# A two-layer graph transformer: one more feed-forward block in seven products, the next layer's keys one chunk later, the last empty attention steps spaced

## The chip, the cores and the metric

The kernel runs on one core of one Trainium2 chip. The time is the device time of one execution, in microseconds (us). Smaller is better. Five engines work side by side, each through its own instructions in their written order: PE (TensorE, matrix products), ACT (ScalarE, activations and copies with a scale), DVE (VectorE, elementwise work and reductions), POOL (GpSimd, here mostly indirect transfers and small powers) and SP (SyncE, here only transfers).

## The reference

There are 2708 tokens of 512 values and a 0/1 adjacency matrix, sparse enough that no token has more than 24 neighbours. Two layers of the same form follow each other; cut to what matters, one is:

```python
q, k, v = ((h @ W.T + b).reshape(n, 8, 64) for W, b in ((Wq, bq), (Wk, bk), (Wv, bv)))
scores = jnp.einsum('nhd,mhd->hnm', q, k) / jnp.sqrt(64.)
scores = jnp.where(mask[None] == 0, -1e9, scores)
ctx = jnp.einsum('hnm,mhd->nhd', jax.nn.softmax(scores, -1), v).reshape(n, 512)
h1 = layer_norm(h + ctx @ Wo.T + bo, ln1_g, ln1_b)
ff = jax.nn.relu(h1 @ W1.T + b1) @ W2.T + b2          # W1: 2048 x 512, W2: 512 x 2048
h2 = layer_norm(h1 + ff, ln2_g, ln2_b)
```

Everything is 32-bit floating point.

## The kernel before, in words

**Tokens and blocks.** The tokens are sorted by their number of neighbours and cut into 22 tiles of 128 (the last, tile 21, holds 20). Two tiles make a block, and a layer runs over 11 blocks, `k` from 0 to 10. The order of the tiles is fixed in a list; the last block holds tile 21 and tile 0, and tile 0 has the longest neighbour lists (22).

**What a block does.** The main loop (L2078 to L2183) takes one block at a time through 16 chunks, `f` from 0 to 15. Chunk `f` computes 128 of the 2048 hidden values for the block's 256 tokens: four products into `pf` on PE (each of 256 columns), then a relu from `pf` to `ft` on ACT. The second matrix is applied some chunks later. The work of other stages is hung on these chunks by hand, so that PE always has something to do. All engines are scheduled by hand: each instruction stands on its engine where the loop issues it.

**Two forms of the second product.** In the plain form (`feed_forward`, L1548) chunk `f-3` is multiplied with its 128 x 512 part of W2 for both tiles: two products of 512 columns per chunk. In the seven-product form (`feed_forward_by_seven`, L1734) two chunks and two tiles make a 2 x 2 block product, done by the Strassen-Winograd scheme: seven products of 256 columns in place of eight. It has 7 such pairs of chunks, `j` from 0 to 6, and the last two chunks in the plain way. `sums(j)` (four DVE operations, L1746 to L1749) forms the sums of the relu outputs that the scheme needs; it is issued in chunk `2j+2`. `products(j)` (L1751) issues the seven products at the end of chunk `2j+5`, that is, after everything else that the loop hangs on that chunk. The first of the seven needs no sums; the second needs the result of L1748. `ask_forms` (L1725) fetches the three preformed pieces of W2 for each pair with transfers on SP. `FORMED = (1, 3)` (L60) says for each layer after which block the seven-product form begins: in layer 0 blocks 2 to 9 have it, in layer 1 blocks 4 to 9. Before it begins, `prepared` (L2086) lays out its buffers in the place of Wq, `form_in` (L2135, L2137) puts one difference of W2's parts in the place of a part of W2, and `places_of_psum` (L2088) goes from three PSUM buffers for `pf` (tag `f`) and three for everything else (tag `g`) to two and two, with two for the sums of products.

**What is hung on the chunks.** In the order of one pass of the loop: first the chunk's own products and relu, and then

- in layer 1, a step of `ended` for the block before (the last layer norm and the store), at the chunks in `TAILS`;
- in layer 0, a step of `keys_values` (L1858) for the block before, at chunks 5, 6, 7 and 8 (L2101, L2102): the first step turns the block's two tiles on PE (`flip`, L1349: transposes into two PSUM buffers `tp` of tag `g`, and four ACT copies for each from there to `zT`, L1354). The second and third step project one tile each to keys and values of layer 1 (L626, 8 + 8 PE instructions, `k` and `v` in the same two PSUM buffers), with a DVE add and an ACT copy, and store `zT` and the tile through SP. The fourth writes the keys and values by an indirect transfer on POOL (`put`);
- at chunks 10 to 14, the output projection and the first layer norm of the next block (`attended`), whose tiles must have come out of the attention by then: `until(...)` (L2106, L2111) forces the rest if they have not;
- at chunk 15 the next block is turned for its own first products;
- `advance` (L2120) runs steps of the attention.

**The attention** (`attend`, L1908) is a generator of steps in the order of the tiles. A step takes up to two neighbours of each token of a tile: `weights` multiplies the gathered keys with the queries and sums over each head (DVE, L1156 and L1162). One step later `weigh` takes the exponentials (ACT, L1175), multiplies the values of the second neighbour by them (8 ACT operations, L1182) and those of the first (DVE, L1188), and adds them up (DVE, L1195). For the last step of a tile, `sums` follows one step after that (DVE, L1203 to L1218) and `divided` another one later (8 ACT operations, L1226, into `cx`). Behind the first block's two tiles and at the end of the layer stand three empty steps that only let this tail run out. Each step has a price, 0.5 or 1 for one or two neighbours and 0.2 for an empty one (L1950); `advance` hands out credit by `PACE` or, in seven-product blocks, `PACE7`, and runs steps while credit is left and fewer than three finished tiles wait.

## Time and profile before

| | |
|---|---|
| median of 3 runs | 1817.57 us (1815.81 to 1818.39) |
| the profiled execution, its time | 1817.08 us |
| its span, first to last instruction | 1815.1 us |
| PE, busy share of the span | 99% |
| DVE, ACT, POOL | 81%, 55%, 47% |

The time of an execution is about 2 us above the span of the same execution, the part before the first and after the last instruction. A busy share is a mean over stages that differ; a busy PE means that some product was under way. Two kinds of view carry the argument. A table of stages gives, for stretches of time, the busy time of each engine; the stretches used here run from the first relu of one block to the first relu of the next, so that each is the length of a block. A timeline lists the instructions of an engine in order of time, like neighbours merged into one row: start, duration, engine, line, operation, out<-in, shapes, count, and in brackets how long the engine had been idle and for what. One matrix product in 32-bit floating point appears as two PE instructions.

### The profile page before, as it was taken

How to read it: one execution, taken by the hardware profiler on the slowest of the kernel's cores; microseconds unless marked ns; L12 is line 12 of the kernel's file. 1: busy time of each engine (PE TensorE's matmuls, PEld its weight loads, DVE VectorE, ACT ScalarE, POOL GpSimd, SP SyncE). 2: the span in 40 equal slices, each digit the busy share in tenths (PEclk: the TensorE clock that was granted, in tenths of full speed). 3: DMA queues.
4: the chain of work that ended last, by engine and by line, in shares of the span. 5: the costliest groups of instructions: out<-in, count | busy, mean ns of one | idle time of the engine just before them, and what ended most of it. 6: DMA issues, size and time to landing. Idle time of an engine off the chain costs nothing. (4 is left out here: it accounts for less than half of the span.)

```text
span 1815.1 us, 23887 instructions
## 1 busy us (share of the span) xinstructions
PE 1791.5 (99%) x6839; PEld 1214.6 (67%) x6839; DVE 1463.3 (81%) x2599; ACT 1001.1 (55%) x3397; POOL 855.4 (47%) x830
## 2 busy tenths in 40 slices
PE   9999999999999999999999999999999999999997
PEld 4444456666777867777677644666666888788786
DVE  4987778988989889799896267988888899989933
ACT  5771436645555555555653104677776677767631
POOL 3333755534454544454540132556665665655312
PEclk9999999999999999999999999999999999999999
DMA  9997987757676675666752777967867787877531
GB/s 335 369 344 252 374 284 245 230 181 241 203 238 220 203 259 192 208 220 202 241 194 73 242 285 272 319 193 256 279 186 263 243 264 237 293 225 234 173 94 36
DMA packets 186728, 426.74 MB, mean 235 GB/s; under 512 B 20550, under 2 KB 83898, under 8 KB 186584
## 3 DMA queue, kind: packets, MB, share of 16 engines
q0 software_dynamic: 76992, 264.49, 44.0%
q1 hardware_dynamic: 99434, 139.01, 22.5%
q10 hardware_dynamic: 10158, 21.61, 3.1%
q8 instruction: 56, 0.92, 0.2%
q14 instruction: 88, 0.72, 0.1%
HBM read 357.13 MB, written 57.11 MB: 228 GB/s over the span
## 5 line engine op out<-in xcount | busy, mean ns | idle before, releaser
L1119 POOL DMA_INDIRECT kv<-kv_d,listed x420 | 526.0, 1252 | 307.2 <-DVE acc L1195 145.8
L1780 PE MATMUL pf<-hT,w 128*128 128x256 f32 x1792 | 407.2, 379 | 2.1 <-ACT ft L1791 2.1
L1780 PEld LDWEIGHTS pf<-hT,w 128*128 128x128 f32 x1792 | 339.2, 190 | 59.2 <-issue 11.0
L1182 ACT ACTIVATE kv<-kv,p 128x64 f32<-128x64 f32 x1232 | 311.0, 335 | 5.0
L1156 DVE TENSOR_TENSOR kv<-kv,q 128x1024 f32<-128x1024 f32 (+1 forms) x222 | 257.1, 1158 | 14.1 <-DMA q<-q_d,ident_i 10.9
L1162 DVE TENSOR_REDUCE sc<-kv 128x16 f32<-128x1024 f32 (+1 forms) x222 | 258.0, 1162 | 7.6
L1195 DVE TENSOR_TENSOR acc<-acc,kv 128x1024 f32<-128x1024 f32 (+2 forms) x178 | 205.6, 1155 | 49.6 <-ACT kv L1182 36.9
L1596 PEld LDWEIGHTS pf<-hT,w 128*128 128x128 f32 x1024 | 178.5, 190 | 55.3 <-issue 34.6
L1596 PE MATMUL pf<-hT,w 128*128 128x256 f32 (+1 forms) x1024 | 214.6, 357 | 0.1
L1791 ACT ACTIVATE ft<-pf,b 128x256 f32<-128x256 f32 x168 | 78.1, 466 | 214.1 <-PE pf L1780 211.4
L1569 PE MATMUL a<-w,ft 128*128 128x512 f32 x416 | 194.6, 592 | 0.0
L1175 ACT ACTIVATE p<-sc,listed 128x8 f32<-128x8 f32 x420 | 103.6, 295 | 127.9 <-DVE sc L1162 116.5
L1281 POOL TENSOR_TENSOR rd<-va,mhalf 128x1 f32<-128x1 f32 (+1 forms) x48 | 43.8, 913 | 230.8 <-DVE va L1279 230.7
L626 PE MATMUL o<-wo,cT 128*128 128x512 f32 x336 | 151.0, 593 | 0.3 <-ACT cT L1354 0.3
L1188 DVE TENSOR_TENSOR kv<-kv,p 128x512 f32<-128x512 f32 (+1 forms) x178 | 123.6, 694 | 4.8 <-ACT p L1175 4.5
L1569 PEld LDWEIGHTS a<-w,ft 128*128 128x128 f32 x416 | 77.7, 190 | 57.5 <-issue 52.0
L626 PEld LDWEIGHTS o<-wo,cT 128*128 128x128 f32 x336 | 63.4, 190 | 69.3 <-issue 59.6
L1331 POOL TENSOR_SCALAR va<-sq 128x1 f32<-128x1 f32 (+1 forms) x40 | 17.2, 429 | 188.4 <-ACT xb L1324 101.9
L751 DVE MAX8 tops<-code 128x8 f32<-128x247 f32 (+2 forms) x242 | 78.8, 400 | 28.0 <-ACT code L746 27.9
L1226 ACT ACTIVATE cx<-acc,su 128x64 f32<-128x64 f32 (+1 forms) x352 | 88.2, 333 | 11.2 <-DVE su L1218 6.2
L1182 ACT ACTIVATE acc<-kv,p 128x64 f32<-128x64 f32 (+1 forms) x352 | 88.8, 335 | 1.4
L746 ACT ACTIVATE code<-aj 128x1354 bf16<-128x1354 int32 (+1 forms) x44 | 73.5, 1724 | 23.7 <-POOL aj L740 19.0
(258 smaller groups left out, 2793.8 us busy)
## 6 DMA issues: line engine op xcount, KB each, us to landing
forms<-form_d SPq DMA_DIRECT2D x294, 128.0 KB, 3.8
aj<-in_adj SPq DMA_DIRECT2D x42, 677.0 KB, 6.3
kv_d<-kvs ACTq DMA_DIRECT2D x21, 512.0 KB, 7.4
h<-ln_b POOLq DMA_DIRECT2D x41, 256.0 KB, 7.0
xg<-in_xT SPq DMA_DIRECT2D x19, 512.0 KB, 8.0
w<-in_W SPq DMA_DIRECT2D x16, 512.0 KB, 6.4
kv<-kv_d,listed POOLq DMA_INDIRECT x420, 6.5
zT_d<-zT SPq DMA_DIRECT2D x22, 256.0 KB, 5.3
```

Source lines behind the costliest of these rows:

```text
L626: nc.tensor.matmul(o[:r], xs(c), wm[:, c, :], start=(c == 0), stop=(c == NC - 1))
L1119: return nc.gpsimd.indirect_dma_start(out=to, out_offset=None, in_=table[:, :], in_offset=bass.IndirectOffsetOnAxis(ap=s, axis=0), bounds_ ...
L1156: nc.vector.tensor_tensor(kv[:r, :c, :DM], kv[:r, :c, :DM], self.q[:r].unsqueeze(1).to_broadcast([r, c, DM]), ALU.mult,)
L1162: nc.vector.tensor_reduce(self.sc[:r, s0 : s0 + c, :], kv[:r, :c, :DM].rearrange("p s (h d) -> p s h d", d=DK), AX.X, ALU.add,)
L1175: nc.scalar.activation(p[:r, s, :], self.sc[:r, s, :], AF.Exp, bias=minus[:r, g, s : s + 1])
L1182: nc.scalar.activation(to[:, i, hd], kv[:r, i, DM + h * DK : DM + (h + 1) * DK], AF.Copy, scale=p[:r, s0 + i, h : h + 1],)
L1188: nc.vector.tensor_tensor(to[:, 0, :].rearrange("p (h d) -> p h d", d=DK), kv[:r, 0, DM:].rearrange("p (h d) -> p h d", d=DK), p[:r, s0, : ...
L1195: nc.vector.tensor_tensor(self.acc[:r, :c, :], self.acc[:r, :c, :], kv[:r, :c, DM:], ALU.add)
L1226: nc.scalar.activation(cx[:r, hd], self.acc[:r, 0, hd], AF.Copy, scale=self.su[:r, h : h + 1])
L1569: nc.tensor.matmul(a[:r, cols], fts[f][:, c0 : c0 + r], self.w2[f // 2][:, f % 2, cols], start=(f == 0), stop=(f == NFC - 1),)
L1596: nc.tensor.matmul(pf[:, :w], self.w1[f // 2][:, c, f % 2 * P : f % 2 * P + P], hT[:, c, :w], start=(c == 0), stop=(c == NC - 1),)
L1780: nc.tensor.matmul(pf[:, :W], self.w1[j][:, c, f % 2 * P : f % 2 * P + P], hT[:, c, :], start=(c == 0), stop=(c == NC - 1),)
```

## The change

Three lines change.

```diff
-FORMED = (1, 3)
+FORMED = (1, 2)
...
             if t3 and t3[-1]:
                 got[t3[0].g] = t3[0].divided()
-            yield c / SLOTS if step else 0.2
+            yield c / SLOTS if step else 0.2 if g == order[1] else 1.0
...
                 if tail and f in TAILS[k > FORMED[n] + 1]:
                     next(tail)
-                if f in (5, 6, 7, 8) and behind:
+                if behind and more <= f - 5 < 4 + more:
                     next(behind)
```

The first lets the seven-product form begin at block 3 of layer 1, its fourth, and moves with it what prepares it: the buffers and the differences of W2 one block earlier (block 2 and the start of block 3), the two PSUM buffers of each kind from block 3 on, and the pace of `PACE7` for the attention in block 3.

The second gives the three empty steps at the end of a layer a price of 1.0 each; those behind the first block keep 0.2.

In the third, `more` is true for all blocks but the last, and counts as 1: the four steps of `keys_values` stand at chunks 6, 7, 8 and 9 in blocks 1 to 9 of layer 0, and at 5 to 8 in block 10 as before. Layer 1 has no such steps.

## The prediction

> **What bounds the kernel now.** I read the page first, then who waited for whom, then the blocks as stages, last the timelines of chunks 4 to 7.

> ```profile
> span 1815.1 us, 23887 instructions
> PE 1791.5 (99%) x6839; PEld 1214.6 (67%) x6839; DVE 1463.3 (81%) x2599; ACT 1001.1 (55%) x3397; POOL 855.4 (47%) x830
> ```

> PE lacks 23.6 us of its span, so a change pays only by fewer products or by fewer of PE's waits, and each new wait of PE is paid in full. One wait that the third edit is about leads the list of PE's waits:

> ```profile
> PE tp L1349 <- DVE h L1290: 3.1, 4, 1.0
> ```

> Layer 0's blocks 2, 3, 4, 5 and 6 as stages (length, then PE busy):

> ```profile
> 395.47:472.05 76.58, 75.73 (x311) 1.00 0.67 219
> 472.05:548.92 76.87, 75.89 (x311) 1.00 0.66 223
> 548.92:624.38 75.46, 75.46 (x311) 1.00 0.68 227
> 624.38:700.88 76.50, 75.71 (x311) 1.00 0.65 212
> 700.88:777.38 76.50, 75.72 (x311) 1.00 0.64 208
> ```

> A block without waits takes 75.46; blocks 2 and 3 lose 1.1 and 1.4.

> **Edit 1, the seven products.** Layer 1's block 3 (plain, now), 4 (seven), 6, 8 and 9 (length, then PE, PEld, DVE, ACT and POOL busy, granted clock, share of the DMA engines):

> ```profile
> 1341.94:1405.65 63.71, 63.71 (x225) 41.13 (x224) 53.23 (x73) 46.55 (x170) 39.05 (x37) 1.00 0.74 251
> 1405.65:1466.49 60.84, 60.84 (x271) 49.87 (x270) 53.97 (x91) 44.72 (x161) 38.01 (x34) 1.00 0.80 262
> 1527.34:1588.91 61.57, 61.24 (x271) 49.77 (x270) 58.37 (x102) 40.86 (x145) 37.37 (x33) 1.00 0.79 257
> 1650.02:1712.80 62.78, 61.82 (x271) 49.60 (x270) 59.92 (x102) 44.75 (x162) 30.41 (x30) 1.00 0.68 219
> 1712.80:1770.85 58.05, 58.05 (x272) 47.60 (x271) 28.53 (x70) 23.50 (x73) 10.37 (x14) 1.00 0.32 78
> ```

> Block 3 goes from 63.71 to 60.84: **-2.9 us**. It takes PE's products over from block 4 as they are: 49 products of 256 columns and four wide ones' worth in place of 32 wide ones of 512, 3.5 wide ones fewer at some 0.86 each. Block 4 is itself the first of its form and pays nothing for the change of buffers. Block 3 adds 28 DVE sums and 21 fetches on SP, and moves seven fetches one block up; DVE (54 of 61) and the transfers (0.80) carry that in block 4. Its pace sums to 10.0 in place of 11.1; by the prices, 10 steps run in block 3 in place of 12, and block 9, where DVE is busy for 28.53 of 58, gets 3 in place of 1. In between every step stands one or two chunks later. Blocks 6 and 8 show what an unlucky place costs, 0.7 and 1.9 over 60.84; shifted steps can lose these 2.7 or find them again: -2.7 to +2.7, and I take 0, as blocks of the same form lie on both sides.

> PEld, the weight loads, grows from 41.13 to 49.87 while the block gets shorter. [...]

> **Edit 3, the keys one chunk later.** What does the turning of the block wait for, and what is next? Block 2, chunk 5:

> ```profile
> 403.91 0.60 PE L1349 MATMUL tp<-ident,h 128*128 128x128 f32 x4
> 405.75 0.28 DVE L1748 TENSOR_TENSOR forms<-forms,ft 128x128 f32<-128x128 f32 x1
> 405.85 0.60 PE L1769 MATMUL a<-forms,ft 128*128 128x256 f32 x2
> ```

> The second tile's turn waits for the block before's layer norm on DVE. Unhindered, as in block 7 below, the first product follows the first turn by 0.87; here by 1.94, in block 3 by 2.07. Removed by the move: 1.07 + 1.20 = **-2.3**. But products(0), issued at the end of chunk 5, now comes in the place of the turn, and needs DVE too: its second product takes the result of L1748, which DVE computes right behind the same layer norm. Nothing makes DVE earlier. Blocks 3, 5 and 8:

> ```profile
> 480.49 0.60 PE L1349 MATMUL tp<-ident,h 128*128 128x128 f32 x4
> 482.45 0.28 DVE L1748 TENSOR_TENSOR forms<-forms,ft 128x128 f32<-128x128 f32 x1
> 482.56 0.60 PE L1769 MATMUL a<-forms,ft 128*128 128x256 f32 x2
> ```

> ```profile
> 632.81 1.04 PE L1349 MATMUL tp<-ident,h 128*128 128x128 f32 x8
> 633.41 0.28 DVE L1748 TENSOR_TENSOR forms<-forms,ft 128x128 f32<-128x128 f32 x1
> ```

> ```profile
> 861.41 1.04 PE L1349 MATMUL tp<-ident,h 128*128 128x128 f32 x8
> 862.14 0.28 DVE L1748 TENSOR_TENSOR forms<-forms,ft 128x128 f32<-128x128 f32 x1
> ```

> Block 7 gives the pace of the array:

> ```profile
> 785.81 1.04 PE L1349 MATMUL tp<-ident,h 128*128 128x128 f32 x8
> 786.68 0.60 PE L1769 MATMUL a<-forms,ft 128*128 128x256 f32 x2
> 789.71 1.89 PE L1780 MATMUL pf<-hT,w 128*128 128x256 f32 x8
> 791.43 3.60 PE L626 MATMUL k<-wk,zT 128*128 128x512 f32 x8
> ```

> Two turns 0.87, seven products 3.03 (0.43 each), a chunk's `pf` 1.72. So the second product is wanted 0.43 after the row of the turn: block 2 at 404.34, L1748 ends at 406.03: 1.7 lost. Block 3: 482.73 - 480.92 = 1.8. Block 5, and 6 which has its length: 633.69 - 633.24 = 0.45 each. Block 8: 862.42 - 861.84 = 0.6. Block 7: none. First waits: **+5.0**. Bounds: 0 if DVE came early, 5.0 as it stands.

> The second thing is ACT's queue. Now the copies of `zT` stand behind the relu of chunk 5 and ahead of chunk 5's attention step. After the change they stand behind that step and the relu of chunk 6. And `k` needs the PSUM buffer that the four copies of the first tile read (two buffers of tag `g`), so all four must be done. Block 7, ACT:

> ```profile
> 787.45 2.14 ACT L1354 ACTIVATE zT<-tp,bo 128x128 f32<-128x128 f32 x8
> 790.01 0.49 ACT L1175 ACTIVATE p<-sc,listed 128x8 f32<-128x8 f32 x2 [0.42 <-DVE sc L1162]
> 792.46 2.00 ACT L1226 ACTIVATE cx<-acc,su 128x64 f32<-128x64 f32 x8
> 794.37 0.45 ACT L1791 ACTIVATE ft<-pf,b 128x256 f32<-128x256 f32 x1
> ```

> The step starts when DVE has its scores, whatever stands ahead of it, and ends with the relu of chunk 6 at 794.82. Four copies take half of 2.14: `zT` is there at 795.9. On PE, `k` comes after products(0), `pf`, two turns, `pf`: 785.81 + 3.03 + 1.72 + 0.87 + 1.72 = 793.15. Lost: 2.7. Today the same copies are ready in time, ahead of the step. Block 8 has the same eight scalings in chunk 5, block 3 has none there:

> ```profile
> 870.59 0.45 ACT L1791 ACTIVATE ft<-pf,b 128x256 f32<-128x256 f32 x1
> ```

> ```profile
> 488.99 0.46 ACT L1791 ACTIVATE ft<-pf,b 128x256 f32<-128x256 f32 x1
> ```

> Block 8: copies done 871.04 + 1.05 = 872.1; PE 861.41 + 7.34 + the 0.6 already lost = 869.35: 2.75. Block 3: 490.5 against 480.49 + 7.34 + 1.8 = 489.65: 0.85. In blocks 2 and 5 the step would start at its scores:

> ```profile
> 408.58 1.22 DVE L1162 TENSOR_REDUCE sc<-kv 128x16 f32<-128x1024 f32 x1
> ```

> ```profile
> 636.25 1.22 DVE L1162 TENSOR_REDUCE sc<-kv 128x16 f32<-128x1024 f32 x1
> ```

> A step without scalings is 2.45 (790.01 to 792.46), relu and copies 0.45 + 1.05: block 2 done at 409.80 + 3.95 = 413.75 against 403.91 + 7.34 + 1.7 = 412.95: 0.8; block 5 at 641.4 against 640.6: 0.8, and 6 the same. Blocks 1, 4, 9 I leave at 0. Second waits: 2.7 + 2.75 + 0.85 + 0.8 x 3 = **+8.7**. Lower bound 0, if ACT came in time; upper bound about +10, if blocks 4 and 9 pay the 0.8 of their neighbours.

> Queues it is moved past: two stores per tile on SP now stand ahead of the fetches of products(1), and wait only for `zT`; `put` on POOL stands behind one more step's gathers and waits for the same ACT copy, the gathers behind it being three steps ahead of use: 0. The last two attention steps of chunk 8 in blocks 5 and 6 keep their distance to the keys' end, so the waits there stay. Edit 3: -2.3 + 5.0 + 8.7 = **+11.4**.

> **Edit 2, the empty steps.** Layer 0, block 9, chunks 9 to 11, and the stage:

> ```profile
> 969.61 1.99 PE L1780 MATMUL pf<-hT,w 128*128 128x256 f32 x8
> 971.18 0.20 DVE L1218 RECIPROCAL su<-su 128x8 f32<-128x8 f32 x1
> 971.42 2.02 ACT L1226 ACTIVATE cx<-acc,su 128x64 f32<-128x64 f32 x8 [2.54 <-DVE flags L1951]
> 974.01 1.52 PE L621 MATMUL o<-wo,cT 128*20 128x512 f32 x8 [2.41 <-ACT cT L1354]
> ```

> ACT stands for 2.54 on the sums of tile 0, and tile 21's copy, behind it, holds PE for 2.41. With the price of 1.0 the three empty steps fall to chunks 8, 10 and 11, the last by force, just ahead of tile 0's own turn. The wait of 2.41 goes; but PE reaches tile 0's turn at 971.4 + 1.5, when the sums, moved behind four DVE operations of 0.28 and a bit, are done at 972.6 and the scalings at 974.6: 1.7. Net **-0.7** (-2.4 to +1). In layer 1 the tail ended at chunk 7 and cost nothing; now, one step later too, it ends at chunk 11: relu 0.45 and scalings 2.0, of which the product of tile 21 covers 1.5, and the drain before the relu: **+1.2** (0 to 2).

> **Sum**: -2.9 + 11.4 - 0.7 + 1.2 = +9.0 on the profiled execution's 1817.08: 1826.1. It lies 0.49 under the median, so **1826.6**.

> **The rivals.**
> *A, the keys move costs nothing (faster).* If DVE's norm at the head of a block ended 2 us earlier, sums and scores would be there and both kinds of waits fall away: 1817.6 - 2.9 - 2.3 + 0.5 = 1812.9. It decides from the point where L1748 ends within 0.43 of the end of chunk 5's products. For it: blocks 4 and 7 are there already. Against it: DVE's chain from the block's end to L1748 has no instruction of the keys in it.
> *B, only the waits on DVE come*, since ACT takes the copies in time: 1826.6 - 8.7 = 1817.9, no change. For it: blocks 2, 3, 5 and 6 hang by 0.8. Against: blocks 7 and 8, by 2.7.
> *C, a long wait slows the array.* Each stretch quoted shows a granted clock of 1.00, with the gap of 2.41 too:

> ```profile
> 928.43:1004.30 75.87, 73.46 (x315) 55.10 (x314) 51.63 (x96) 30.62 (x111) 14.08 (x12) 1.00 0.34 110
> ```

> Two waits of 2.7 are the first longer ones inside layer 0's blocks. If each brought as much again: 1826.6 + 5.4 = 1832. [...]
> *D, edit 1 does not do what it says*: block 3 finds the waits of blocks 6 and 8 too, 2.6 over 60.84, and its gain is gone: 1829.

> **How the numbers follow.** About 0.2% (3.6 us) is what a measurement of this kernel can tell from no change. The forecast has 0.62, with its own range 1821.5 to 1830.5 from the bounds of edit 1 and the second waits. A 0.16, B 0.13, C 0.04, D 0.05. A lies beyond 0.2% faster, B within, the others slower; a tail of the forecast falls within: faster 0.17, same 0.15, slower 0.68. The range reaches from 1814.5, above A, to 1830.

> **What would show it.** In layer 0's blocks 2, 3, 5, 6, 8: `c<-forms` waits for DVE L1748, and no turn waits for L1290. In blocks 7 and 8, `k` waits 2.7 for ACT `zT`, and they last some 78 and 79. Layer 1's block 3 lasts 60.8. Tile 0's turn waits for `cx` in block 9 of both layers. I am wrong if layer 0's seven-product blocks are together no longer than before.

## The result, and the profile after

The changed kernel takes 1833.01 us (median of 6 runs, 1830.73 to 1834.81), the kernel before 1817.49 beside it. The ratio is 1.008, with an interval of 1.007 to 1.0091: 15.5 us slower. The forecast was +9.0, with a range that ended at 1830. The direction was right and the size too small, by 6.5 us, and the time lies 3.0 beyond the end of the range.

The profiled execution of the changed kernel is its fastest one, 1830.73, and lies 13.65 above that of before (1817.08). Its page, the span and the engines:

```profile
span 1828.7 us, 24082 instructions
PE 1792.7 (98%) x6885; PEld 1221.8 (67%) x6885; DVE 1474.0 (81%) x2633; ACT 1002.1 (55%) x3398; POOL 864.7 (47%) x830
```

PE is busy for 1.2 us more and lacks 36.0 us of its span in place of 23.6. The change has made waits. Who waited for whom, PE (microseconds in total, times, longest):

```profile
PE k L626 <- ACT zT L1354: 7.5, 8, 2.4
PE tp L1349 <- ACT h L1340: 4.1, 4, 1.9
PE c L1769 <- DVE forms L1748: 2.9, 4, 1.7
...
PE c L1769 <- issue: 1.6, 1, 1.6
...
PE tp L1349 <- DVE h L1290: 1.3, 2, 0.6
PE tp L1349 <- ACT cx L1226: 1.0, 3, 0.6
```

Row 1 (`k` for the copies of `zT` on ACT) and rows 3 and 4 (the second of the seven products for L1748 on DVE) are the two new waits that the prediction named for the keys (row 4 is block 2's wait for L1748, which the trace puts down to no engine). The turn's wait for L1290 has gone from 3.1 to 1.3, and tile 0's turn waits for `cx`. Row 2 was not forecast: in layer 1, the turn of the next block's tiles waits for `scaled` (L1340), the last step of the first layer norm, on ACT; it was 0.7 before.

Layer 0's blocks 2, 3, 7, 8 and 9 as stages (start and end, length, then PE, PEld, DVE, ACT and POOL busy, granted clock, share of the DMA engines, GB/s):

```profile
394.99:473.16 78.17, 76.01 (x311) 56.54 (x310) 66.57 (x111) 40.58 (x151) 36.12 (x30) 1.00 0.66 216
473.16:551.46 78.30, 76.04 (x311) 56.56 (x310) 69.64 (x120) 40.59 (x151) 37.02 (x30) 1.00 0.65 215
783.31:861.65 78.34, 75.90 (x311) 56.56 (x310) 69.73 (x112) 44.88 (x170) 40.29 (x31) 1.00 0.69 223
861.65:940.55 78.90, 75.99 (x311) 56.65 (x310) 67.94 (x117) 42.62 (x160) 34.79 (x30) 1.00 0.59 191
940.55:1015.22 74.67, 73.65 (x312) 54.55 (x311) 51.30 (x95) 30.77 (x111) 14.31 (x12) 1.00 0.35 111
```

Blocks 5 and 6 last 78.04 each. Blocks 2 to 8 have become 12.6 longer together. Layer 1's blocks 3, 4, 6 and 9:

```profile
1352.17:1413.83 61.66, 61.23 (x271) 49.79 (x270) 54.01 (x94) 40.35 (x143) 36.32 (x35) 1.00 0.77 248
1413.83:1476.96 63.13, 61.24 (x271) 49.79 (x270) 56.76 (x95) 44.57 (x161) 34.90 (x33) 1.00 0.79 255
1538.08:1601.40 63.32, 61.50 (x271) 49.72 (x270) 59.14 (x102) 42.68 (x153) 36.44 (x33) 1.00 0.68 227
1724.77:1784.55 59.78, 58.78 (x273) 47.72 (x272) 36.77 (x79) 28.27 (x93) 10.00 (x14) 1.00 0.32 85
```

Block 3 gains 2.05 by the seven products, but block 4 loses 2.29 and block 6 1.75. Blocks 3 to 8 are 1.7 longer together, where 2.9 less was forecast.

The account of the span, from the first relu of one block to that of the next: layer 0's blocks 2 to 8 +12.6, its block 9 -1.2, layer 1's blocks 3 to 8 +1.7, its block 9 +1.7, everything else -1.3, together 13.6. The remaining 1.9 up to the medians' 15.5 stands in no row of this execution.

### The profile page after: what moved, and what is told of

The parts are those of the page before. It is cut to its first block, busy times and chain, and to the rows that moved or that the text cites. A ratio compares the mean times of both kernels' runs of the same rounds, so it can differ in the third digit from the quotient of the medians.

```text
span 1828.7 us, 24082 instructions
## 1 busy us (share of the span) xinstructions
PE 1792.7 (98%) x6885; PEld 1221.8 (67%) x6885; DVE 1474.0 (81%) x2633; ACT 1002.1 (55%) x3398; POOL 864.7 (47%) x830
## 4 chain that ended last, share of the span: by engine, by line
PE 75%; DVE 12%; ACT 6%; issue 4%; DMA 2%; POOL 1%; POOLq 0%; SPq 0%; DVEq 0%; ACTq 0%
PE pf L1780 14%; PE k L626 8%; PE v L626 8%; PE pf L1596 8%; PE q L626 7%; PE o L626 7%; PE c L1769 7%; PE a L1569 7%; PE a L1769 5%; ACT kv L1182 3%; DVE kv L1156 2%; DVE sc L1162 2%; PE tp L1349 2%; PE a L1800 1%; PE a L1804 1%
## 5 line engine op out<-in xcount | busy, mean ns | idle before, releaser
L1119 POOL DMA_INDIRECT kv<-kv_d,listed x420 | 533.1, 1269 | 317.5 <-DVE acc L1195 134.1
L1780 PE MATMUL pf<-hT,w 128*128 128x256 f32 x1920 | 437.7, 380 | 2.8 <-ACT ft L1791 2.8
L1780 PEld LDWEIGHTS pf<-hT,w 128*128 128x128 f32 x1920 | 362.9, 190 | 63.0 <-issue 11.5
L1162 DVE TENSOR_REDUCE sc<-kv 128x16 f32<-128x1024 f32 (+1 forms) x222 | 257.9, 1162 | 7.6
L1195 DVE TENSOR_TENSOR acc<-acc,kv 128x1024 f32<-128x1024 f32 (+2 forms) x178 | 205.5, 1155 | 56.5 <-ACT kv L1182 44.6
L1791 ACT ACTIVATE ft<-pf,b 128x256 f32<-128x256 f32 x180 | 83.4, 465 | 210.3 <-PE pf L1780 210.3
L1596 PE MATMUL pf<-hT,w 128*128 128x256 f32 (+1 forms) x896 | 184.9, 355 | 0.1
L1175 ACT ACTIVATE p<-sc,listed 128x8 f32<-128x8 f32 x420 | 103.9, 296 | 143.9 <-DVE sc L1162 133.1
L1569 PE MATMUL a<-w,ft 128*128 128x512 f32 x352 | 164.9, 593 | 0.0
L626 PE MATMUL o<-wo,cT 128*128 128x512 f32 x336 | 151.2, 594 | 0.3 <-ACT cT L1354 0.3
L626 PEld LDWEIGHTS o<-wo,cT 128*128 128x128 f32 x336 | 63.3, 190 | 68.8 <-issue 57.4
L1569 PEld LDWEIGHTS a<-w,ft 128*128 128x128 f32 x352 | 65.6, 190 | 48.2 <-issue 43.6
L1226 ACT ACTIVATE cx<-acc,su 128x64 f32<-128x64 f32 (+1 forms) x352 | 88.2, 333 | 8.7 <-DVE su L1218 8.6
```

The lines of the kernel that those rows point to most:

```text
L626: nc.tensor.matmul(o[:r], xs(c), wm[:, c, :], start=(c == 0), stop=(c == NC - 1))
L1119: return nc.gpsimd.indirect_dma_start(out=to, out_offset=None, in_=table[:, :], in_offset=bass.IndirectOffsetOnAxis(ap=s, axis=0), bounds_ ...
L1162: nc.vector.tensor_reduce(self.sc[:r, s0 : s0 + c, :], kv[:r, :c, :DM].rearrange("p s (h d) -> p s h d", d=DK), AX.X, ALU.add,)
L1175: nc.scalar.activation(p[:r, s, :], self.sc[:r, s, :], AF.Exp, bias=minus[:r, g, s : s + 1])
L1195: nc.vector.tensor_tensor(self.acc[:r, :c, :], self.acc[:r, :c, :], kv[:r, :c, DM:], ALU.add)
L1569: nc.tensor.matmul(a[:r, cols], fts[f][:, c0 : c0 + r], self.w2[f // 2][:, f % 2, cols], start=(f == 0), stop=(f == NFC - 1),)
```

## The experiments

**Each edit alone.** The edit to the seven products, to the keys, to the empty steps, one at a time:

```diff
-FORMED = (1, 3)
+FORMED = (1, 2)                                                        # form_alone
...
-                if f in (5, 6, 7, 8) and behind:
+                if behind and more <= f - 5 < 4 + more:                # keys_alone
...
-            yield c / SLOTS if step else 0.2
+            yield c / SLOTS if step else 0.2 if g == order[1] else 1.0 # empty_alone
```

> Only the first edit: block 3 of layer 1 in seven products, keys and empty steps as before. Theory P (the steps' new places are what costs in layer 1): layer 0 as before; layer 1's blocks 3 to 8 together +1.7 us over the kernel before, as in the changed kernel (61.7, 63.1, 61.1, 63.3, 60.8, 62.5); block 9 +1.5 to +2.5, because the three cheap empty steps now run out together at chunk 9; some 1821 us in all, slower than before by 3 to 4.5. Rival N (places are neutral, as predicted): 1814.6.

> Only the third edit: layer 0's keys at chunks 6 to 9. Theory: the waits of layer 0 are the keys' alone: blocks 2 to 8 +12.6 us as in the changed kernel, block 9 about +0.4, layer 1 as before: 1830 to 1831. Rival (the waits need the other edits): within 3 us of 1817.5.

> Only the second edit: the last three empty steps at a price of 1.0. Theory: layer 0's block 9 loses the wait of 2.4 for tile 21's copy and gets a shorter one, some -1.2 to -1.6; layer 1, where the attention ends at chunk 9 in place of 7, gets nothing: 1816.1. Rival as predicted (a wait of 1.7 takes its place, -0.7): 1816.8; rival (the wait only moves): 1817.5.

Beside a kernel before of 1817.65: the seven products alone 1824.8 (ratio 1.0031, 1.0022 to 1.004), the keys alone 1830.83 (1.007, 1.0056 to 1.0084), the empty steps alone 1816.31 (0.9991, 0.9982 to 1.0). The first came 3.8 above its theory's 1821, the other two as their theories had it. By the medians, the edit that removes 3.5 wide products makes the kernel 7.2 slower, the keys cost 13.2, and the empty steps gain 1.3. These differences add up to 19.0 where the three together cost 15.5. The ratios, taken times the time before, say less of each: 5.6, 12.7 and -1.6, together 16.7, for 14.5. So the three don't simply add up, and by how much they miss is known only roughly. The gain of the empty steps is at the edge of what the measurement can tell, since its interval ends at 1.0.

Layer 1's blocks 3 and 4 last 61.31 and 64.88 with the seven products alone, block 6 63.66, so the loss in layer 1 does not need the keys. (Block 4's 64.88 is 1.75 above the changed kernel's 63.13. This run's profiled execution was its slowest, 1828.76, at a mean clock of 0.995 for the changed kernel's 0.998, so some of it is probably time at half the clock, which is taken up below; that is an estimate.) In the run of the keys alone blocks 2 to 6 last what they last in the changed kernel, to 0.01, and layer 1's blocks are as before, to 0.3. PE's waits of that run are the changed kernel's rows 1 and 3 to 0.1: `k` waits 7.6 for `zT` in 8 places, and the products wait 2.9 for L1748 in 4. Blocks 7 and 8 of that run, though, are 1.6 and 1.7 longer than the changed kernel's with the same waits:

```profile
783.07:863.04 79.97, 77.52 (x311) 57.16 (x310) 69.85 (x112) 45.02 (x169) 40.28 (x31) 0.98 0.68 219
863.04:943.64 80.60, 77.69 (x311) 57.18 (x310) 68.02 (x117) 42.66 (x159) 34.77 (x30) 0.98 0.58 188
```

PE is busy 77.5 in place of 75.9, and the granted clock is 0.98. That is taken up below.

**All but the keys.** The first and the third of these edits in one kernel.

> The change without the move of the keys. Theory: the two other edits add up as in the changed kernel; layer 1's blocks 3 to 9 as there (+3.5 over before), layer 0's block 9 1.5 shorter, and no wait of over 2.2 is left, so no half clock: about 1819.5. Rival (the keys' move also caused the waits of layer 1 by shifting what reaches the transfers): layer 1's blocks 4 and 6 come back to 60.8 and the time is about 1814.

1820.17 (ratio 1.0015, 1.0003 to 1.0027) beside 1817.59. Layer 1's blocks 3, 4, 5, 6, 7 and 9 last 61.32, 64.81, 61.12, 63.68, 60.84 and 59.78, and layer 0's block 9 is 1.57 shorter: the loss is layer 1's own, the rival is out. That no stretch at half clock would be left was wrong: one follows block 4's wait of 1.89 (a clock of 0.50 from 1452.93 to 1456.35), and block 4's 64.81 holds it. Block 9 of layer 1 also explains part of the missing additivity: with the empty steps spaced and nothing else it takes 58.05, as before; with the seven products alone `o` waits there 2.48 for `cT`, and the block takes 61.08; with both edits it takes 59.78. So the seven products' shift costs 3.0 there, and the spaced steps give 1.3 of it back.

**What layer 1 loses.** The seven-product form runs the attention by another pace, so in block 3 its steps fall in other chunks, and every later step of the layer moves with them. The changed kernel at the end of block 4, ACT and the turn on PE (start, duration, engine, line, and in brackets the idle time before and what ended it):

```profile
1457.90 0.72 ACT L1324 ACTIVATE xb<-h,nm 128x512 f32<-128x512 f32 x1 [4.63 <-DVE nm L1318]
...
1461.41 2.00 ACT L1226 ACTIVATE cx<-acc,su 128x64 f32<-128x64 f32 x8
1463.32 0.45 ACT L1791 ACTIVATE ft<-pf,b 128x256 f32<-128x256 f32 x1
1463.68 1.32 ACT L1340 ACTIVATE h<-h,rd 128x512 f32<-128x512 f32 x2
1464.44 1.27 PE L1349 MATMUL tp<-ident,h 128*128 128x128 f32 x8 [1.89 <-ACT h L1340]
```

The same place in the kernel before:

```profile
1447.48 0.72 ACT L1324 ACTIVATE xb<-h,nm 128x512 f32<-128x512 f32 x1 [0.94 <-DVE nm L1318]
...
1452.68 0.47 ACT L1791 ACTIVATE ft<-pf,b 128x256 f32<-128x256 f32 x1 [1.58 <-PE pf L1780]
1453.05 1.32 ACT L1340 ACTIVATE h<-h,rd 128x512 f32<-128x512 f32 x2
1454.20 1.04 PE L1349 MATMUL tp<-ident,h 128*128 128x128 f32 x8
```

Two things have come together. First, ACT's first operation of the norm that `scaled` ends (L1324) gets its sum from DVE later: it begins 44.06 after the block's first relu in place of 41.83, since on DVE two attention steps and the sums of a finished tile now lie between the norms of the two tiles, where one step lay before. Second, a tile's end, `divided` (L1226, 2.00), has come to stand ahead of `scaled` (L1340) in ACT's order, where ACT had 1.58 of rest before. Now PE waits 1.89. In block 6 ACT's order is the old one, and the first alone has happened:

```profile
1584.24 0.72 ACT L1324 ACTIVATE xb<-h,nm 128x512 f32<-128x512 f32 x1 [6.42 <-DVE nm L1318]
```

That is 46.17 after the block's first relu in place of 44.41, and the turn waits 1.41. If the places of the steps are the cause, credit given at other chunks must take these waits away with the same products on PE. Two tries, both by adding to the pace in a few chunks of layer 1:

```diff
+EXTRA = {(1, 1, 11): 0.3, (1, 2, 11): 0.6, (1, 3, 11): -0.3, (1, 3, 12): 0.5}   # form_paced
+EXTRA = {(1, 2, 11): 1.1, (1, 3, 11): -0.3, (1, 3, 12): 0.3}                    # form_paced2
...
-                advance((PACE7 if seven else PACE if k else PACES)[n][f])
+                advance((PACE7 if seven else PACE if k else PACES)[n][f] + EXTRA.get((n, k, f), 0.0))
```

> The first edit, and credit of 0.3 more at chunk 11 of layer 1's block 1, 0.6 more at chunk 11 of block 2, 0.3 less at chunk 11 and 0.5 more at chunk 12 of block 3, so that by the prices every attention step of blocks 4 to 9 stands at the chunk where it stood in the kernel before. Theory P: blocks 4 to 9 as before (60.8, 60.8, 61.6, 61.1, 62.8, 58.1), block 3 60.8 to 61.5: 1814.6 to 1815.3, faster than before by 2.2 to 2.9. Rival R (the seven-product form in block 3 itself disturbs the blocks behind it, through buffers or transfers): as slow as with the first edit alone, 1818 or more.

> As form_paced, but the added credit of layer 1 all at chunk 11 of block 2 (1.1), and 0.3 moved from chunk 11 to 12 in block 3: chunks 0 to 10 of block 2 as in the kernel before, so that the scaling of tile 6 stays behind the copies for the output projection; blocks 4 to 9 as before by the prices. Theory P: block 2 at 63.7 to 64.5, block 3 at 60.8 to 61.5, the rest as before: 1814.7 to 1816, faster than before by 1.5 to 2.9. Rival R (DVE has no room for the two steps before block 4, wherever they stand): block 2 or 3 longer by 2 or more, 1817.5 or more.

The first gave 1819.43 (ratio 1.0008, 0.9999 to 1.0017): blocks 4 to 9 are no longer than before, to 0.05, but another `divided` fell in front of the copies of `cT` in block 2, where `o` waited 2.31 and the clock fell (0.97 on the mean of 1276.90 to 1345.00). That is 4 above its theory. The second gave 1816.34 (0.9989, 0.998 to 0.9998) beside 1818.27, 0.3 above its theory's range. Its blocks 3 and 4 of layer 1:

```profile
1342.04:1404.52 62.48, 62.48 (x278) 50.91 (x276) 54.79 (x94) 42.74 (x153) 37.21 (x35) 1.00 0.83 267
1404.52:1464.95 60.43, 60.18 (x268) 49.07 (x267) 57.36 (x97) 45.15 (x163) 37.82 (x34) 1.00 0.76 255
```

The waits are gone, with the same 6885 instructions on PE, and ACT's operation on the late sum is back at 41.93 and 44.26 in blocks 4 and 6. Blocks 3 to 8 are 2.0 shorter than before, where the changed kernel's are 1.7 longer. So the seven products bring 2.0 of the 2.9 that they promise, and the place of the steps decides over 3.7 us. Which of the two things costs how much in block 4 was not tried apart. The first edit also moves something that the description of the change does not list: `TAILS` is chosen by `FORMED` too, so block 4's five steps of `ended` go from chunks 1, 2, 3, 5 and 8 to 3, 4, 5, 6 and 9. Both tries have them there as well and lose nothing in block 4, so they are not the cause.

**What the keys lose: two ways round.** If ACT's order holds the copies of `zT` back, the projections can be put later, or the turn left where it was:

```diff
-                if f in (5, 6, 7, 8) and behind:
+                if behind and f in ((5, 7, 8, 9) if more else (5, 6, 7, 8)):    # keys_split
+                if behind and f in ((6, 8, 9, 10) if more else (5, 6, 7, 8)):   # keys_late
```

> Only layer 0's keys are moved: the turn stays at chunk 5, the two projections go to chunks 7 and 8, the store to 9 (blocks 1 to 9). Theory Q (two queues: products(0) in the turn's place waits for DVE, and zT's copies stand behind chunk 5's attention step on ACT): with the turn at its old place both waits are gone and the old ones for the layer norm are back: layer 0's blocks within 0.3 us of the kernel before, 1817.5 in all. Rival (the later projections and their stores are what costs): some 1826 to 1830.

> Only layer 0's keys are moved: turn at chunk 6, projections at 8 and 9, store at 10 (blocks 1 to 9). Theory Q: zT's copies get 11 us more, the eight waits of k for zT are gone, the waits of products(0) for L1748 stay (1.7, 1.8, 0.4, 0.4, 0.5 in blocks 2, 3, 5, 6, 8): blocks 2 to 8 at 77.2, 77.3, 75.5, 75.9, 75.9, 75.5, 76.0, since the waits of 0.8 in blocks 5 and 6 at chunk 11 go too; block 9 without the wait of 2.4, some 73.5: 1815 to 1817. Rival (the keys' place is bad as such, the later the worse): over 1830.

Both missed their theory. The turn early, the projections one chunk later: 1821.42 (ratio 1.0018, 1.0009 to 1.0027), between the theory and the rival. Turn one chunk late and everything after it two: 1835.9 (1.009, 1.0075 to 1.0106), on the side of the rival. PE's waits, first of the former, then of the latter:

```profile
PE k L626 <- ACT kvs L1886: 3.6, 3, 1.8
PE tp L1349 <- DVE h L1290: 3.1, 4, 1.0
...
PE k L626 <- ACT zT L1354: 0.2, 1, 0.2
```

```profile
PE k L626 <- ACT kvs L1886: 12.1, 5, 5.1
PE c L1769 <- DVE forms L1748: 2.9, 4, 1.7
...
PE k L626 <- ACT zT L1354: 0.3, 1, 0.3
```

The waits for `zT` are gone in both, as the theory had it, and with the turn at its old place those for L1748 are gone too and the 3.1 for L1290 are back. In their place the second tile's `k` waits for the copies that empty the PSUM buffers of the first, which now stand behind further attention steps on DVE and ACT. In the first of the two runs, block 3:

```profile
492.51 3.60 PE L626 MATMUL v<-wv,zT 128*128 128x512 f32 x8
...
500.42 0.69 DVE L1195 TENSOR_TENSOR acc<-acc,kv 128x512 f32<-128x512 f32 x1
...
501.19 0.58 ACT L1886 COPY kvs<-v 128x512 f32<-128x512 f32 x1 [5.06 <-PE pf L1780]
501.21 0.69 DVE L1881 TENSOR_TENSOR kvs<-k,bk 128x512 f32<-128x512 f32 x1
...
501.83 2.41 PE L626 MATMUL k<-wk,zT 128*128 128x512 f32 x5 [0.97 <-ACT kvs L1886]
```

`v` ends at 496.1 and is copied 5 us later, although ACT is idle. The copy and the add begin within 0.02 of each other, 0.1 behind the last reading of gathered rows (L1195). In the code `kvs` comes from the same five buffers as those rows (tag `kv`), so it may have waited for one of them; that is argued from the code and was not tried by itself.

**The turn late, the attention step behind it.** The last way: the keys as in the change, but in layer 0's blocks 3 to 8 the credit of chunk 5 is handed out in chunk 6, behind the copies of `zT`; blocks 7 and 8 get 0.6 and 0.3 more at chunk 9; block 2 stays as it is for comparison.

```diff
+LATER = {3: 0.6, 4: 0.6, 5: 0.6, 6: 0.6, 7: 0.9, 8: 0.6}
+EXTRA = {(0, k, f): (2 * f - 11) * x for k, x in LATER.items() for f in (5, 6)}
+EXTRA |= {(0, 7, 9): 0.6, (0, 8, 9): 0.3}
```

> The keys one chunk later alone, and in layer 0's blocks 3 to 8 the attention step of chunk 5 is issued in chunk 6, behind the copies of `zT` on ACT; block 2 keeps its step in chunk 5. Theory (the copies of `zT` wait in ACT's order behind that step): in blocks 3 to 8 the waits of `k` for `zT` (6.9 in the run of the keys alone, the two of 2.4 among them) go, block 2 keeps its 0.5, the waits for L1748 (2.9 and 1.6) stay; with the two stretches at half clock gone too, about 1821. Rival (the copies are late for another reason: the turn itself or the buffer): the waits stay and the time is about 1830. Second rival (the step, now in chunk 6, holds DVE's and ACT's copies of k and v back in its turn): waits of `k` for `kvs` appear and the time is 1825 or more.

1835.45 (ratio 1.009, 1.0068 to 1.0111), where the theory had 1821. PE's waits (the lines are 3 higher in this kernel):

```profile
PE c L1772 <- DVE forms L1751: 11.0, 5, 3.6
...
PE k L629 <- ACT zT L1357: 1.1, 3, 0.5
```

Of the waits for `zT`, 0.5 is left in block 2 and none in blocks 3 to 8: ACT's order was their cause. But the waits for L1748 (L1751 here) went from 2.9 to 11.0, which no theory had. They grew in blocks 4, 5 and 8 alone (1.90, 3.41 and 3.60), and these are the blocks behind those in which a moved step pushed another one from chunk 10 to chunk 13: DVE begins that step 16.0 before the end of blocks 3, 4 and 7, in place of 31. The steps behind it then run into the end of the block, ahead of the sums and the layer norm that close it: those of block 4 begin on DVE (L1826 here) 2.43 after block 5's first relu, where in the run of the keys alone they began 0.62 before it. The difference, 3.05, is what the wait in block 5 grew by (3.41 for 0.35):

```profile
637.16 0.59 PE L1772 MATMUL a<-forms,ft 128*128 128x256 f32 x2
...
640.83 0.28 DVE L1751 TENSOR_TENSOR forms<-forms,ft 128x128 f32<-128x128 f32 x1
...
641.16 0.70 PE L1772 MATMUL c<-forms 128*128 128x256 f32 x2 [3.41 <-DVE forms L1751]
```

This is read from the two traces; no run moved that step back by itself.

**The parts that pay, together.** The seven products with the second pace, and the empty steps spaced in layer 0 only:

```diff
+            yield c / SLOTS if step else 0.2 if n > 0 or g == order[1] else 1.0
```

> form_paced2, and the empty steps at the end of layer 0 alone at a price of 1.0. Theory: the gains add up, -2.2 from layer 1 and -1.3 to -1.6 from layer 0's block 9, and no episode of half clock: 1813.5 to 1814.5. Rival R: 1816 to 1817.

1814.18 (ratio 0.9979, 0.9969 to 0.999) beside 1818.27, as the theory had it: 4.1 faster than before by the medians, and the lowest time and ratio of this study.

## Why the prediction was right or wrong

**The keys' waits: right, in place and nearly in size.** The first waits (DVE, L1748) were put at 5.0 and measured 4.5: 1.65 and 1.72 in blocks 2 and 3, 0.34, 0.34 and 0.47 in 5, 6 and 8. The second waits (`k` for `zT`) were put at 8.7 and measured 7.3, of which 0.3 is in block 9, where none was forecast. Block 7, where the forecast was 2.7:

```profile
798.39 2.00 ACT L1226 ACTIVATE cx<-acc,su 128x64 f32<-128x64 f32 x8
800.30 0.45 ACT L1791 ACTIVATE ft<-pf,b 128x256 f32<-128x256 f32 x1
800.65 2.12 ACT L1354 ACTIVATE zT<-tp,bo 128x128 f32<-128x128 f32 x8
801.82 3.70 PE L626 MATMUL k<-wk,zT 128*128 128x512 f32 x8 [2.44 <-ACT zT L1354]
```

The order is the one worked out: scalings, relu, copies, `k`. The 0.8 that was put on blocks 2, 5 and 6 came as 0.52 to 0.54. The seven blocks together came out at +12.6 for +11.4, since PE's busy time in them grew as well, by 0.15 to 0.54 a block: products that start behind a wait show longer rows here (3.70 at 801.82 above, for 3.60 in the kernel before; 0.70 for 0.59 at 641.16, with the turn late and the attention step behind it). Rivals A and B fall, A because both kinds of waits came, B because those on ACT did. The two later tries bear the mechanism out: with the turn at its old place both kinds of waits are gone, and with the attention step behind the copies those for `zT` are gone.

**The empty steps: right in layer 0, the right size by luck in layer 1.** Tile 0's turn waits for `cx` in both layers, as forecast. Layer 0's block 9 came at -1.2 for -0.7, because this wait is 0.28 there and not 1.7. Layer 1's block 9 came at +1.7 for +1.2, but that is not a price of these steps: by themselves they leave the block at 58.05. It is what is left of the 3.0 that edit 1's shift costs there.

**Edit 1: wrong, and this is the step that failed.** It said: "shifted steps can lose these 2.7 or find them again: -2.7 to +2.7, and I take 0, as blocks of the same form lie on both sides". The products did become fewer by what was said. The shift was no coin with two equal sides: in block 4 it made DVE's sum for the norm late and put `divided` ahead of `scaled` on ACT (1.89), and in block 6 it made DVE's sum late (1.41). Even the bound of 2.7 was too narrow: +1.7 lies 4.6 from -2.9, as several blocks paid at once. Rival D named this loss, but in block 3; it came in 4 and 6. What could have been seen: the order of DVE's and ACT's instructions follows from the credit by arithmetic, step by step, for all 7 blocks; the prediction counted the steps of each block and did not place them.

**The clock: wrong.** The forecast gave rival C 0.04, because the gap of 2.41 showed a clock of 1.00. But no run shows that a wait of this length leaves the clock alone wherever it falls. The changed kernel waits 2.44 in block 8, the run of the keys alone 2.4 in the same place. Stretches are laid end to end here from the trace's first record of the clock, each as long as the two at 0.50 in the run of the keys alone (801.47:804.88 and 883.39:886.80), 3.41. The one that holds most of the wait and the one behind it, in the changed kernel and in the run of the keys alone (length, then the engines, the granted clock behind POOL's count):

```profile
879.04:882.46 3.42, 1.68 (x4) 0.87 (x5) 3.18 (x8) 3.39 (x15) 0.99 (x1) 1.00 0.55 181
882.46:885.87 3.41, 3.41 (x9) 1.52 (x8) 3.27 (x5) 2.26 (x10) 1.17 (x2) 1.00 0.86 268
```

```profile
879.97:883.39 3.42, 1.22 (x3) 0.68 (x4) 3.18 (x7) 3.42 (x15) 1.00 (x2) 1.00 0.43 144
883.39:886.80 3.41, 3.41 (x5) 1.33 (x4) 3.27 (x5) 2.70 (x11) 1.45 (x2) 0.50 0.90 275
```

In the changed kernel the wait is cut in two by the border of the stretch, PE works 1.68 of 3.42, and the clock stays at 1.00; in the keys alone it lies almost whole in one, PE works 1.22 of 3.42, and the next stretch is granted 0.50: five PE instructions in place of nine. Block 8 lasts 80.60 there for 78.90, so such a stretch costs 1.7 here. The gap of 2.41 that the forecast leaned on had been cut in the same way: its larger part lies in a stretch in which PE works 1.85 of 3.41 (969.76 to 973.17 of the kernel before), and the next one is at 1.00.

**Where the 6.5 went**, then: edit 1's shifted steps 4.6, the keys 1.2, the two blocks 9 together nothing, elsewhere -1.3 (differences in the first part and the transition between the layers that no experiment looked into), and 1.9 that the profiled execution doesn't show. For these the stretches at half clock are the likely place: at 1.7 each, some one more in the median execution would do. That is an estimate, and it is not shown: the other executions left no trace in which such stretches could be counted. Their mean clocks point the same way. Of the changed kernel's six, the two at 0.998 took 1830.73 and 1832.53, the three at 0.997 1832.85 to 1834.13, the one at 0.996 1834.81. Of the five of the keys alone, the three at 0.998 took 1829.33 to 1830.83, the two at 0.996 1832.58 and 1833.05, and the first of these two is the profiled one, with two such stretches.

## What to carry to other kernels

When a piece of work is moved by one place in hand-ordered queues, write down for every engine it touches what then stands ahead of each of its instructions, and do this for the attention-like work that shifts along as well, block by block; "on average nothing" was the one term that failed, and it was worth more than the gain. A wait that is filled by moving work hands its cause to the next reader: here each of the four other arrangements of the keys cost time, through one queue or another (DVE's sums, ACT's copies, the emptying of PSUM, the norm at the block's end). And a wait of PE can cost more than its length: here the 2.4 of block 8 came with 1.7 on top in the run of the keys alone, and without it in the changed kernel.

## What the runs showed of the hardware

| run | first stretch | PE busy in it | granted clock of the next |
|---|---|---|---|
| the turn late, the attention step behind it | 638.83:642.24 | 1.07 | 0.50 |
| the keys alone | 798.05:801.47 | 1.10 | 0.50 |
| the keys alone | 879.97:883.39 | 1.22 | 0.50 |
| all but the keys | 1449.52:1452.93 | 1.52 | 0.50 |
| the keys alone | 985.79:989.20 | 1.60 | 1.00 |
| the turn late, the attention step behind it | 990.40:993.81 | 1.60 | 1.00 |
| the changed kernel | 879.04:882.46 | 1.68 | 1.00 |
| the changed kernel | 1462.72:1466.14 | 1.70 | 1.00 |
| the kernel before | 969.76:973.17 | 1.85 | 1.00 |
| the changed kernel | 800.54:803.95 | 2.13 | 1.00 |

The closest two, the kernel without the move of the keys (block 4 of layer 1) and the keys alone (layer 0's block 9):

```profile
1449.52:1452.93 3.41, 1.52 (x9) 0.87 (x8) 3.17 (x8) 3.41 (x12) 2.63 (x3) 1.00 0.57 149
1452.93:1456.35 3.42, 3.42 (x11) 2.88 (x12) 2.93 (x3) 3.39 (x14) 2.74 (x2) 0.50 0.96 333
```

```profile
985.79:989.20 3.41, 1.60 (x8) 1.07 (x6) 2.35 (x10) 2.19 (x9) 0.00 (x0) 1.00 0.00 0
989.20:992.61 3.41, 3.00 (x17) 1.91 (x18) 1.37 (x3) 2.06 (x10) 0.00 (x0) 1.00 0.02 5
```

PE busy for 1.52 of 3.41 was followed by 0.50, PE busy for 1.60 by 1.00. Whether other waits fall out the same way was not shown. The wait of 2.4 in block 8 stands on both sides, with PE busy for 1.68 in the changed kernel and for 1.22 in the keys alone. The seven products alone, with four waits of 1.96 to 2.57, ran between 1820.76 (mean clock 0.998) and 1828.76 (0.995). The empty steps alone, with no wait over 1.5 after the start, ran between 1812.95 and 1818.12, all at 0.998, so a spread of 5 has other causes.
